# An LSTM's input operands on GpSimd beside first steps, weight sums queued in program order, and an output one gate later

## The chip, the cores and the metric

The kernel runs on one core of one Trainium2 chip. The metric is the device time of one execution in microseconds (us). A core has a matrix engine (TensorE, PE in the profile; its weight loads are PEld), a vector engine (VectorE, DVE), a scalar engine (ScalarE, ACT), a third elementwise engine (GpSimd, POOL) and a queue engine (SyncE, SP) that only issues transfers here. Each engine works through its own instructions in order; an instruction that waits for another engine or a transfer holds up all that stand behind it on its engine.

## The reference

The input x has 128 x 64 nodes of 256 features, all in float32. Four layers follow each other, each in the form x = x + layer(relu(layernorm(x))). The change lies in the first. After two graph convolutions that layer runs four LSTMs in turn, with window lengths p = 1 to 4:

```
for p in range(1, MAX_SKIP + 1):
    nw = Tv // p
    wins = h[:, :nw * p, :].reshape(Bv * nw, p, Hd)
    last = _lstm_last(Wih[p - 1], Whh[p - 1], bih[p - 1], bhh[p - 1], wins)
    idx = jnp.arange(nw) * p + (p - 1)
    h = h.at[:, idx, :].set(last.reshape(Bv, nw, Hd))
```

One step of an LSTM computes g = x_t @ Wih.T + h @ Whh.T + bias, splits g into the gates i, f, g, o, and then c = sigmoid(f) * c + sigmoid(i) * tanh(g) and h = sigmoid(o) * tanh(c). The state is zero at the start, so the first step has no h product and needs no gate f. The second layer is an attention over 512 edges, the third a graph convolution with batch norms, the fourth a dense attention.

## The kernel before

The 8192 tokens are four groups (g) of 2048. The LSTMs run over two halves: groups 0 and 1 through all four window lengths, then groups 2 and 3. Within a half a window length w is a phase; there are eight phases, numbered 0 to 7. A phase is a list of steps (class `Step`, L595): a part of a group, and a time t below w. Two parts are interleaved, so that the steps go first part t=0, second part t=0, first part t=1, and so on. A step has N columns: 512 for w=1, 256 for w=2 and 4, 336 for w=3.

A gate is a 2x2 block product done with seven products instead of eight (`gate`, L686; `product`, L644). Operand x[1] to x[7] of the seven are column blocks and sums of them. A step at t=0 has 3 gates of 7 products, a later step 4 gates of 14, since the state's seven products with Whh come on top. The profile holds a product as two matmul records. A gate goes through PSUM tiles pa (3 buffers), pb (2, shared with the transposes' `bank`) and pc (3); ScalarE copies pa (L694, L699) and pc (L702, for t=0 on VectorE), VectorE adds (L695, L705, L710), ScalarE applies the functions (L679, L732). `gate_done` (L714) makes the cell c (L728, L729, L731) and h with its own sums (L750 to L754), or writes the last h back into the node array hT (L737, L745).

The operands of a step are made by `prepare` (L617). For w above 1 these are two copies on ScalarE (L632 of two blocks, L633 of one) and three subtractions on VectorE (L634 of two blocks, L640 and L641 of one) into a tile xop with two buffers. The node array is read with a stride of w elements.

The main loop (L820) runs over slots, one gate per slot. Three gates are in flight: in a slot the new gate issues its first two products, the gate of two slots ago its last two, the gate of one slot ago its fifth, and the new gate two more. The next step's `prepare` is called beside the last gate but one of a step; for a new half's first step it is beside the last gate.

The weights (class `Weights`, L424) are a transfer of 1 MB on SP (L429) and four subtractions or additions on GpSimd (L440), giving tiles wih, sih for the input and whh, shh for the state. When a phase is over, `phase_over` (L806) loads the state weights of the next phase at once, and enters the input weights of the phase after next into a list that is served eight slots later (L863). wih has two buffers, whh one.

When a group is through w=4, `group_out` (L779) writes it out in two chunks (c = 0, 1): 16 transposes on PE (L167), four additions to the residual tiles xres on VectorE (L172), a store to xa on GpSimd's queue (L786), and, for the first half's groups, the loads of the next half's nodes hmem into hT on SP (L789). The main loop calls it one slot and two slots after the group's last gate. The residual tiles (4 buffers) are fetched on SP (L772). Outputs that are left when the slots end go into `last_outs` (L883); the attention layer then fetches their residuals (L919) and writes one of them out in each call of `edges` (L290). After the second call the pools of the LSTM's arrays are closed (L321) and the third layer's weights are loaded.

The order of each engine's instructions is not the program's alone: a planner takes them as its own estimate of the times lets them become ready. `late(ins)` ties an instruction behind the one that stands before it on its engine in the program. The first matmul of each group of products is tied in this way, so PE keeps the program's order; `prepare`, `Weights` and most of `gate` are not tied.

Of the kernel before, what the change touches and what calls it, by code (L numbers as in the profile page):

```python
# [13 lines left out]
ALU = mybir.AluOpType  # L14
# [3 lines left out]
T = 64  # L18
# [12 lines left out]
def gnn_stack_kernel(ctx: ExitStack, tc: tile.TileContext, a: dict, out: bass.AP):  # L31
    nc = tc.nc
# [45 lines left out]
    class Norm:  # L78


        def __init__(self, xt, root_on_scalar=False, keep=late):
            self.xt, self.root_on_scalar, self.keep, self.h = xt, root_on_scalar, keep, None
            self.st = stat.tile([P, 4, 6], F32, tag="ln_st", name="ln_st")
            self.mv = stat.tile([P, 4, 2], F32, tag="ln_mv", name="ln_mv")
# [170 lines left out]
    keep = tabs.tile([P, E], F32, tag="keep", name="keep")  # L255
# [159 lines left out]
    with ExitStack() as l0:  # L415
# [6 lines left out]


        class Weights:  # L424
            def __init__(self, kind, w):
                bufs = 2 if kind == "ih" else 1
                t = wsp.tile([P, 2, 4, 2, P], F32, tag=f"w{kind}", name=f"w{kind}", bufs=bufs)
                s = wsp.tile([P, 3, 4, P], F32, tag=f"s{kind}", name=f"s{kind}", bufs=bufs)
                nc.sync.dma_start(  # L429
                    out=t.rearrange("p k q j m -> p k (q j m)"), in_=a[f"W{kind}T"][:, w - 1]  # L430
                )
                a11, a12, a21, a22 = t[:, 0, :, 0, :], t[:, 1, :, 0, :], t[:, 0, :, 1, :], t[:, 1, :, 1, :]
                s1, s2, s4 = s[:, 0], s[:, 1], s[:, 2]
                for o, x, y, op in (
                    (s1, a21, a22, ALU.add),
                    (s2, s1, a11, ALU.subtract),
                    (s4, a12, s2, ALU.subtract),
                    (a21, a11, a21, ALU.subtract),
                ):
                    nc.gpsimd.tensor_tensor(o, x, y, op)  # L440
                self.of = {1: a11, 2: a12, 3: s4, 4: a22, 5: s1, 6: s2, 7: a21}

            def __call__(self, k, q):
# [6 lines left out]
        weights = {}  # L450


        with ExitStack() as conv:
# [43 lines left out]
            p = bank()  # L497
# [97 lines left out]
        class Step:  # L595
# [18 lines left out]
            def as_nodes(self, ap):  # L614
                return ap.rearrange("p q (b n) -> p q b n", n=self.nw) if self.w == 3 else ap

            def prepare(self):  # L617

                N, t = self.N, self.t
                x = xop.tile([P, 7 * NMAX], F32, tag="x", name="xop")  # L620
                if self.w == 1:
                    v = x[:, : 4 * N].rearrange("p (q n) -> p q n", n=N)
                    nc.vector.tensor_tensor(
                        v[:, 0:2], self.nodes(slice(2, 4), 0), self.nodes(slice(0, 3, 2), 0), ALU.subtract
                    )
                    b11, b21, b22 = (self.nodes(slice(k, k + 1), 0)[:, 0] for k in (0, 1, 3))
                    nc.vector.tensor_tensor(v[:, 2], b22, v[:, 0], ALU.subtract)
                    nc.vector.tensor_tensor(v[:, 3], b21, v[:, 2], ALU.subtract)
                    self.x = {1: b11, 2: b21, 3: b22, 4: v[:, 3], 5: v[:, 0], 6: v[:, 2], 7: v[:, 1]}
                    return  # L630
                v = x[:, : 7 * N].rearrange("p (q n) -> p q n", n=N)
                nc.scalar.copy(self.as_nodes(v[:, 0:2]), self.nodes(slice(0, 2), t))  # L632
                nc.scalar.copy(self.as_nodes(v[:, 2:3]), self.nodes(slice(3, 4), t))  # L633
                nc.vector.tensor_tensor(  # L634
                    self.as_nodes(v[:, 3:5]),
                    self.nodes(slice(2, 4), t),
                    self.nodes(slice(0, 3, 2), t),
                    ALU.subtract,
                )
                nc.vector.tensor_tensor(v[:, 5], v[:, 2], v[:, 3], ALU.subtract)  # L640
                nc.vector.tensor_tensor(v[:, 6], v[:, 1], v[:, 5], ALU.subtract)  # L641
                self.x = {1: v[:, 0], 2: v[:, 1], 3: v[:, 2], 4: v[:, 6], 5: v[:, 3], 6: v[:, 5], 7: v[:, 4]}

            def product(self, q, targets):  # L644
# [112 lines left out]
        steps, phases = [], []  # L757
        for half in range(2):
            ga, gb = 2 * half, 2 * half + 1
            for w in range(1, MAX_SKIP + 1):  # L760
                ph = len(phases)
# [54 lines left out]
        flight = []  # L816
        later, outs = [], []
        norm_steps = iter(())
        steps[0].prepare()
        for slot in range(len(tasks) + 2):  # L820
            new = tasks[slot] if slot < len(tasks) else None
            if slot == len(tasks):

                for _ in norm_steps:
                    pass
                first_hT = gp.tile([P, 4 * NMAX], F32, tag="gate", name="hT1_first")
                first_hT = first_hT[:, : 2 * CHUNK].rearrange("p (c t) -> p c t", c=2)
                for ip in range(2):
                    transpose_features(norms1[0].h, first_hT, ip, late)
            if new:  # L830
                step = steps[new[0]]
                one = step.gate(new[1])
                next(one)
            if len(flight) > 1:
                old = flight.pop(0)
                next(old[1], None)
                next(flight[-1][1])
            elif flight and not new:
                old = flight.pop(0)
                next(old[1], None)  # L840
            else:
                old = None
                if flight:
                    next(flight[-1][1])
            if new:
                next(one)
                flight.append((new, one))
                at, k = new[0], new[2]
                while outs and outs[0][0] <= slot:
                    group_out(*outs.pop(0)[1:])  # L850

                new_half = at + 1 < len(steps) and at and steps[at + 1].w == 1 < step.w
                if k == len(step.gates) - (1 if new_half else 2) and at + 1 < len(steps):
                    steps[at + 1].prepare()
                if step.w == MAX_SKIP and step.t == 2 and k < 2 and step.g < NGR - 1:
                    for u in range(2):
                        n = 4 * step.g + 2 * u + k
                        later.append((slot, "x", n))
            while later and later[0][0] <= slot:
                _, kind, n = later.pop(0)  # L860
                residual[n] = fetch_x(n)
            next(norm_steps, None)
            while later_weights and later_weights[0][0] <= slot:  # L863
                _, ph = later_weights.pop(0)
                weights["ih", ph] = Weights("ih", phases[ph])
            if old:
                (at, q, k), step = old[0], steps[old[0][0]]
                if k == len(step.gates) - 1:
                    if at + 1 == len(steps) or steps[at + 1].phase != step.phase:
                        phase_over(step.phase)  # L870
                    if step.phase == len(phases) - 1 and step.t == 1 and step.g == NGR - 1:

                        t_ = wsp.tile([P, 2, 4, 2, P], F32, tag="wih", name="x_first", bufs=2)
                        flat = t_.rearrange("p k q j m -> p k (q j m)")
                        norms1 = {}
                        for n in range(2):
                            xt = flat[:, n, :].rearrange("p (i d) -> p i d", i=4)
                            nc.sync.dma_start(out=xt, in_=xa[n])
                            norms1[n] = Norm(xt)
                        norm_steps = first_norms1(norms1)  # L880
                    if step.w == MAX_SKIP and step.t == MAX_SKIP - 1:
                        outs += [(slot + 1, step.g, 0), (slot + 2, step.g, 1)]
        last_outs = [(g, c) for _, g, c in outs]  # L883
    psums["banks"] = None

# [2 lines left out]
    with ExitStack() as l1:  # L888
# [306 lines left out]
        def sums(n, xt, keep=False):  # L1195

            st = stat.tile([P, 4, 6], F32, tag="ln_st", name="ln_st")
            mv = stat.tile([P, 4, 2], F32, tag="ln_mv", name="ln_mv")
            for i in range(4):
                ins = nc.vector.bn_stats(st[:, i, :], xt[:, i, :])  # L1200
                if keep and i == 0:
                    late(ins)
                nc.vector.bn_aggr(mv[:, i, :], st[:, i, :])
            rs, nm = w12t["x_rs"][:, n, :], w12t["x_nm"][:, n, :]
            ins = nc.gpsimd.tensor_scalar(rs, mv[:, :, 1], 1e-5, None, ALU.add)
            if keep:
                late(ins)
            nc.gpsimd.tensor_tensor(rs, rs, half_power, ALU.pow)
            nc.gpsimd.tensor_tensor(nm, mv[:, :, 0], rs, ALU.mult)
            nc.gpsimd.tensor_scalar(nm, nm, -1.0, None, ALU.mult)  # L1210
# [782 lines left out]
```

## Time and profile before

| what | value |
|---|---|
| median of 3 runs | 2067.21 us (2066.95 to 2071.63) |
| the profiled execution's own time | 2061.03 us |
| span of that execution | 2059.3 us |
| mean granted TensorE clock | 0.996 |
| first to last matmul of the LSTMs (L651) | 192.8 to 1273.5 us |
| PE busy in the span | 2006.1 us (97%) |
| POOL busy in the span | 308.2 us (15%) |

The span runs from the first to the last instruction; 1.7 us of the execution lie around it. A row such as `418.83 0.49 DVE L705 ...` is an instruction's start, its duration, its engine, its line in the kernel, what it writes and reads, and how many follow one another; in brackets stand the engine's idle time before it and what ended it. A wait such as `PE pa L651 <- DVE gate L705: 8.2, 11, 1.6` says that matmuls into pa waited for the instruction of L705, 8.2 us in all, 11 times, at most 1.6 us. The table by stages gives for each window the busy time and count for every engine, the clock and the share of the transfers' engines.

### The profile page before, as it was taken

How to read it: one execution, taken by the hardware profiler on the slowest of the kernel's cores; microseconds unless marked ns; L12 is line 12 of the kernel's file. 1: busy time of each engine (PE TensorE's matmuls, PEld its weight loads, DVE VectorE, ACT ScalarE, POOL GpSimd, SP SyncE). 2: the span in 40 equal slices, each digit the busy share in tenths (PEclk: the TensorE clock that was granted, in tenths of full speed). 3: DMA queues.
4: the chain of work that ended last, by engine and by line, in shares of the span. 5: the costliest groups of instructions: out<-in, count | busy, mean ns of one | idle time of the engine just before them, and what ended most of it. 6: DMA issues, size and time to landing. Idle time of an engine off the chain costs nothing. (4 is left out here: it accounts for less than half of the span.)

```text
span 2059.3 us, 25491 instructions
## 1 busy us (share of the span) xinstructions
PE 2006.1 (97%) x9444; PEld 1346.1 (65%) x9444; DVE 1359.5 (66%) x2507; ACT 1184.4 (58%) x2230; POOL 308.2 (15%) x416
## 2 busy tenths in 40 slices
PE   8999999999999999999999999999999999999998
PEld 6777478866688845887667887333334775444786
DVE  8755666564565477566556555677777877886776
ACT  4344766555565457566446564666675556591544
POOL 3000010020110020002001000323223420000563
PEclk9999999999999999999999999999999999999999
DMA  9331000100100170001001003412223841022012
GB/s 316 98 98 51 0 21 1 42 0 1 41 1 1 40 246 21 1 0 42 0 1 41 1 16 120 138 61 97 72 98 122 298 154 52 0 82 82 32 62 72
DMA packets 63196, 135.06 MB, mean 66 GB/s; under 512 B 6240, under 2 KB 40928, under 8 KB 60768
## 3 DMA queue, kind: packets, MB, share of 16 engines
q1 hardware_dynamic: 56832, 109.11, 15.6%
q0 software_dynamic: 5632, 24.12, 3.1%
q8 instruction: 74, 1.21, 0.2%
q14 instruction: 50, 0.41, 0.1%
q10 hardware_dynamic: 608, 0.20, 0.0%
HBM read 87.28 MB, written 46.14 MB: 65 GB/s over the span
## 5 line engine op out<-in xcount | busy, mean ns | idle before, releaser
L651 PE MATMUL pa<-xop,sih 128*128 128x256 f32 (+2 forms) x1056 | 344.4, 418 | 11.7 <-DVE gate L705 8.2
L679 ACT ACTIVATE gate<-gate,bias 128x256 f32<-128x256 f32 (+2 forms) x368 | 247.4, 679 | 173.6 <-DVE gate L695 91.0
L651 PEld LDWEIGHTS pa<-xop,sih 128*128 128x128 f32 x1056 | 198.4, 190 | 87.9 <-issue 22.8
L651 PE MATMUL pc<-xop,wih 128*128 128x256 f32 (+2 forms) x736 | 251.2, 423 | 0.0
L695 DVE TENSOR_TENSOR gate<-pb,gate 128x256 f32<-128x256 f32 (+2 forms) x184 | 87.5, 475 | 225.7 <-PE pb L651 154.1
L651 PE MATMUL pa<-lstm_h,shh 128*128 128x256 f32 (+1 forms) x672 | 212.7, 398 | 0.0
L993 DVE SCALAR_TENSOR_TENSOR lr<-lr 128x1024 f32<-128x1024 f32 x128 | 151.1, 1222 | 55.3 <-ACT lr L992 55.3
L651 PEld LDWEIGHTS pc<-xop,wih 128*128 128x128 f32 x736 | 139.8, 190 | 51.2 <-issue 23.0
L710 DVE TENSOR_TENSOR gate<-pc,gate 128x256 f32<-128x256 f32 (+2 forms) x184 | 87.6, 476 | 121.2 <-PE pc L651 120.9
L992 ACT COPY lr<-pair 128x1024 f32<-128x1024 f32 x128 | 123.1, 1014 | 47.6 <-PE pair L986 47.6
L651 PEld LDWEIGHTS pa<-lstm_h,shh 128*128 128x128 f32 x672 | 127.7, 190 | 30.2
L651 PE MATMUL pc<-lstm_h,whh 128*128 128x256 f32 (+1 forms) x448 | 141.8, 398 | 0.0
L694 ACT COPY gate<-pa 128x256 f32<-128x256 f32 (+2 forms) x184 | 76.1, 413 | 96.7 <-PE pa L651 96.1
L986 PE MATMUL pair<-sd_hot,xq 64*128 64x512 f32 x512 | 127.5, 616 | 0.3 <-ACT lr L992 0.3
L705 DVE TENSOR_TENSOR gate<-pa,gate 128x256 f32<-128x256 f32 (+2 forms) x184 | 87.5, 475 | 44.0 <-PE pa L651 43.4
L970 PE MATMUL bank<-wlv,hT 128*128 128x512 f32 x240 | 110.7, 604 | 0.0
L699 ACT COPY gate<-pa 128x256 f32<-128x256 f32 (+2 forms) x184 | 75.4, 410 | 59.1 <-PE pa L651 57.9
L679 ACT ACTIVATE gate<-pa,bias 128x256 f32<-128x256 f32 (+2 forms) x184 | 94.0, 511 | 23.6 <-PE pa L651 22.0
L440 POOL TENSOR_TENSOR sih<-wih 128x512 f32<-128x512 f32 x8 | 10.7, 1335 | 630.6 <-DMA wih<-in_WihT 484.4
L651 PE MATMUL pa<-xop,wih 128*128 128x256 f32 (+1 forms) x320 | 101.4, 398 | 2.7 <-ACT xop L632 2.7
L651 PE MATMUL pb<-xop,wih 128*128 128x256 f32 (+1 forms) x320 | 100.3, 398 | 0.4 <-DVE gate L695 0.4
L651 PEld LDWEIGHTS pc<-lstm_h,whh 128*128 128x128 f32 x448 | 85.1, 190 | 20.1
(346 smaller groups left out, 3809.2 us busy)
## 6 DMA issues: line engine op xcount, KB each, us to landing
field<-sd_hot SPq DMA_DIRECT2D x4, 2304.0 KB, 17.2
wih<-in_WihT SPq DMA_DIRECT2D x8, 1024.0 KB, 5.1
xres<-in_x SPq DMA_DIRECT2D x16, 512.0 KB, 4.6
xa<-xres POOLq DMA_DIRECT2D x16, 512.0 KB, 5.2
dense<-field POOLq DMA_DIRECT2D x4, 2048.0 KB, 8.5
xin<-xb SPq DMA_DIRECT2D x16, 512.0 KB, 3.4
h<-xb SPq DMA_DIRECT2D x16, 512.0 KB, 3.2
xin<-in_x SPq DMA_DIRECT2D x15, 512.0 KB, 3.9
```

The costliest lines, as they stand in the source:

```text
L440: nc.gpsimd.tensor_tensor(o, x, y, op)
L651: ins = nc.tensor.matmul(p[:, : self.N], weights[kind, self.phase](k, q), x[k], start=first_ and kind == "ih", stop=kind == "hh" or not se ...
L679: nc.scalar.activation(out, in_, AF.Tanh if q == 2 else AF.Sigmoid, bias=bias[:, self.w - 1, 2 * q + j : 2 * q + j + 1],)
L694: nc.scalar.copy(blk[0, 0], pa[:, :N])
L695: nc.vector.tensor_tensor(blk[0, 0], pb[:, :N], blk[0, 0], ALU.add)
L699: nc.scalar.copy(blk[1, 0], pa[:, :N])
L705: nc.vector.tensor_tensor(blk[1, 1], pa[:, :N], blk[1, 1], ALU.add)
L710: nc.vector.tensor_tensor(blk[1, 0], pc[:, :N], blk[1, 0], ALU.add)
L970: ins = nc.tensor.matmul(p, hTs[n][:, k, i * P : (i + 1) * P], wlv[:, k, :], start=k == 0, stop=k == 1)
L986: ins = nc.tensor.matmul(p[:, par, :], queries[it][r, c * P : (c + 1) * P], sd_hot[r, :], start=True, stop=True)
L992: nc.scalar.copy(lr, p)
L993: nc.vector.scalar_tensor_tensor(lr, lr, 0.2, lr, ALU.mult, ALU.max)
```

## The change

Three things change.

First, `prepare` is told the step beside which it runs. When that step has t=0 and w above 1, all five instructions are issued on GpSimd. The one exception is the second part's first step for w=3 and w=4 (its nodes come from the step just finished), which stays on ScalarE and VectorE. This moves the operands of 12 steps: for w=2 those of the second part's first step and of the first part's second step (four pairs of parts, 8 steps), for w=3 and w=4 those of the first part's second step (4 steps).

Second, the input weights that are served from the list are tied behind what precedes them on their engines: the load on SP and the four sums on GpSimd.

Third, a group's second chunk goes out three slots after its last gate, not two. For group 2 that slot is the first one past the last gate, where the loop writes nothing out; its second chunk is therefore left in `last_outs`, which holds three entries instead of two, and its two residual tiles are fetched again.

```
-                nc.sync.dma_start(
-                    out=t.rearrange("p k q j m -> p k (q j m)"), in_=a[f"W{kind}T"][:, w - 1]
+                keep(
+                    nc.sync.dma_start(
+                        out=t.rearrange("p k q j m -> p k (q j m)"), in_=a[f"W{kind}T"][:, w - 1]
+                    )
                 )
...
-                    nc.gpsimd.tensor_tensor(o, x, y, op)
+                    keep(nc.gpsimd.tensor_tensor(o, x, y, op))
...
-            def prepare(self):
+            def prepare(self, beside):
...
+                apart = beside is not None and beside.t == 0 and beside.w > 1
+                if apart and self.w > 2 and t == 0:
+                    apart = False
...
-                nc.scalar.copy(self.as_nodes(v[:, 0:2]), self.nodes(slice(0, 2), t))
-                nc.scalar.copy(self.as_nodes(v[:, 2:3]), self.nodes(slice(3, 4), t))
-                nc.vector.tensor_tensor(
+                copy = nc.gpsimd.tensor_copy if apart else nc.scalar.copy
+                sums = (nc.gpsimd if apart else nc.vector).tensor_tensor
+                copy(self.as_nodes(v[:, 0:2]), self.nodes(slice(0, 2), t))
+                copy(self.as_nodes(v[:, 2:3]), self.nodes(slice(3, 4), t))
+                sums(
                     self.as_nodes(v[:, 3:5]),
...
-                nc.vector.tensor_tensor(v[:, 5], v[:, 2], v[:, 3], ALU.subtract)
-                nc.vector.tensor_tensor(v[:, 6], v[:, 1], v[:, 5], ALU.subtract)
+                sums(v[:, 5], v[:, 2], v[:, 3], ALU.subtract)
+                sums(v[:, 6], v[:, 1], v[:, 5], ALU.subtract)
...
-                    steps[at + 1].prepare()
+                    steps[at + 1].prepare(step)
...
-                weights["ih", ph] = Weights("ih", phases[ph])
+                weights["ih", ph] = Weights("ih", phases[ph], late)
...
-                        outs += [(slot + 1, step.g, 0), (slot + 2, step.g, 1)]
+                        outs += [(slot + 1, step.g, 0), (slot + 3, step.g, 1)]
```

More of the change, by code (lines that the diff above doesn't have):

```diff
@@ L424, in gnn_stack_kernel, with __init__ @@
         class Weights:
-            def __init__(self, kind, w):
+            def __init__(self, kind, w, keep=lambda ins: None):
                 bufs = 2 if kind == "ih" else 1
@@ L818, in gnn_stack_kernel @@
         norm_steps = iter(())
-        steps[0].prepare()
+        steps[0].prepare(None)
         for slot in range(len(tasks) + 2):
```

## The prediction

> **What bounds the kernel now.** I read the page's first part, then the waits of PE over the LSTM stretch (192 to 1274 us), then a table by stages of the steps that the change touches, then the time line inside the worst.
>
> ```profile
> PE 2006.1 (97%) x9444; PEld 1346.1 (65%) x9444; DVE 1359.5 (66%) x2507; ACT 1184.4 (58%) x2230; POOL 308.2 (15%) x416
> ```
>
> PE is the bound of the whole, so an edit is worth what it takes from PE's idle time, at most 53 us everywhere. The waits of PE in the LSTMs:
>
> ```profile
> PE pa L651 <- DVE gate L705: 8.2, 11, 1.6
> PE bank L167 <- DVE xres L172: 5.3, 6, 3.1
> PE pa L651 <- ACT gate L694: 3.1, 4, 1.2
> PE pa L651 <- ACT xop L632: 2.7, 2, 1.3
> ```
>
> Few and short; weight loads behind the same gates add to them. Where they fall, the table by stages shows (window, length, then busy time and count of PE, PEld, DVE, ACT, POOL, clock, transfers):
>
> ```profile
> 264.00:275.10 11.10, 10.70 (x44) 7.61 (x43) 10.06 (x19) 9.56 (x18) 1.62 (x2) 1.00 0.28 95
> 333.40:342.40 9.00, 9.00 (x43) 7.88 (x42) 7.99 (x16) 6.76 (x16) 0.00 (x0) 1.00 0.00 0
> 342.40:351.80 9.40, 9.34 (x43) 7.90 (x43) 8.83 (x21) 7.77 (x18) 0.00 (x0) 1.00 0.01 3
> 412.70:427.00 14.30, 12.52 (x44) 7.77 (x43) 13.52 (x19) 9.55 (x17) 9.82 (x6) 1.00 0.00 0
> 565.80:577.40 11.60, 10.00 (x43) 7.65 (x42) 11.07 (x20) 7.81 (x17) 7.91 (x5) 1.00 0.00 1
> 712.20:734.60 22.40, 18.95 (x84) 13.44 (x83) 13.12 (x20) 6.43 (x13) 2.38 (x4) 0.92 0.79 258
> ```
>
> Each of the first five is one step at t=0. A product of 256 columns starts every 0.43 us (0.565 at 336), so 21 products want 9.03 us (11.86). What a window is longer than that is PE lost. DVE is busy 13.52 of 14.30 us and 11.07 of 11.60: in these steps VectorE sets the pace. Steps at t>0 run at pace (24.17 against 24.04).
>
> ```profile
> 416.73 2.17 DVE L634 TENSOR_TENSOR xop<-hT 128x672 f32<-128x672 f32 x1
> 417.90 2.15 POOL L440 TENSOR_TENSOR whh<-whh 128x512 f32<-128x512 f32 x1
> ...
> 421.40 1.57 DVE L640 TENSOR_TENSOR xop<-xop 128x336 f32<-128x336 f32 x1
> ...
> 426.29 0.83 PE L651 MATMUL pa<-xop,sih 128*128 128x336 f32 x2 [1.56 <-DVE gate L705]
> ```
>
> The operands stand in VectorE's queue ahead of the gate's additions, and each takes longer than alone (1.10 and 0.49 us) because GpSimd's weight sums run beside it.
>
> ```profile
> 720.61 1.23 DVE L623 TENSOR_TENSOR xop<-hT 128x1024 f32<-128x1024 f32 x1 [3.48 <-DMA hT<-hm]
> 724.89 1.25 PE L167 MATMUL bank<-ident,hT 128*128 128x128 f32 x8 [3.10 <-DVE xres L172]
> 725.98 1.64 PE L651 MATMUL pa<-hT,wih 128*128 128x512 f32 x2
> ```
>
> At the half's end VectorE waits for a load of new nodes, the output's additions stand behind, the output's second eight transposes find no bank, and after that idle time the clock is at half for 3.4 us (0.92 over the window).
>
> **Part one, the operands.** Excess over pace, first and second half: w=2, first pair of steps 2.1 and 2.9 (after 0.86 that the preceding step ends early); second pair 0.4 and 0.4; w=3, second first step, 2.4 and 2.4; w=4 likewise 2.6 and 1.9. Sum 15.1 us, the ceiling.
>
> Removed in a step at 256 columns: 1.1 us of ScalarE (0.66 and 0.43) and 1.5 of VectorE (0.68, 0.42, 0.41); at 336 columns 1.84 and, as the trace has them, 4.23 (2.17, 1.57, 0.49); at w=4 1.80 and 2.92 (2.10 and two of 0.41).
>
> Added on GpSimd: a 128x512 sum is 1.27 us (weights), a 128x256 one 0.72 (L136), a 128x512 one-input pass 0.77 (L1744), 128x256 0.56 (L1782): 0.77+0.56+1.27+0.72+0.72 = 4.0 us, 5.3 at 336 columns; with the longest rows (2.59 and 1.79 for sums, 1.08 and 0.84 for passes) 8.1. No row has GpSimd on strided nodes; these are the bounds, and I take 5 us, nearer the undisturbed rows. Is it in time? The buffer comes free when the last products of two steps ago are done, some 4.7 us into the step (338.1 in that of 333.4); the first two blocks are wanted 4.3 us later and the fifth product's block 6 us later. The copies are ready after 1.3 us, that block after 3.3 (six at the longest). So ScalarE's and VectorE's work gives way to work that is hidden; uncovered, 1 to 2 us a step.
>
> GpSimd also takes time from VectorE. Rows of before: of VectorE's two-SBUF-input work beside weight sums, L634 took 1.05 more, L640 up to 1.07, L731 0.11 to 0.65, L750 0.26 to 0.77; the additions that read PSUM (L695, L705, L710, L172) 0.00 to 0.03. What stays on VectorE and is exposed are L731 and the four of h, at 0.33 a time by the ten overlapped rows of L731 and L750; about half overlap, some 0.8 us a step against 1.5 to 4.2 removed. The Trainium skill, "GPSIMD Engine Reference", section Key points, says that GpSimd shares its SBUF interfaces with VectorE and contends with VectorE instructions that have two SBUF inputs. By that rule the trace agrees (2.17 against 1.10 us), and it speaks against the change; the first rival carries it.
>
> I take: w=2 first pairs 3.0 of 5.0 (thin margin on VectorE), second pairs nothing, w=3 4.0 of 4.8, w=4 3.4 of 4.5. Together 10.4; the ends are all of the 15.1, and the first rival's loss.
>
> **Part two, the weights.** At a phase's end the GpSimd queue now does the state's four sums first, then the operands, then the four input sums in a t=1 step, where VectorE has time. Before, eight sums run through both t=0 steps at the ends of phases 1, 2 and 5. At the end of phase 6 there are four alone, and that w=4 first step lost 2.8 instead of 3.8: 1.0 us gained once. The load of wih moves behind that of whh on SP; it is wanted a phase later (over 100 us; after phase 3 about 40, or 8 if the tie really holds it eight gates). The sums wait on GpSimd for that load with nothing urgent behind: the next operands come 30 us or more later. Cost 0; bounds 0 to 1 per phase end for VectorE held in the next step.
>
> **Part three, the second output.** Group 0: transposes at 720.75 to 725.98 move behind the next gate's products, whose nodes landed at 720.6. Kept are 2.5 us of transposes (as at 745.73); saved are 5.2-2.5 = 2.7 and 1.8 of clock (22.4 x 0.08), 4.5. Late next: the load into the second chunk, issued at 722 to 727, now at about 728 to 730, landing in 3.5 to 9.5; the next prepare read it at 736.9. VectorE may wait there up to 3.5, PE 0 to 2.5; I take 1.0, so 3.5 net. Group 1: nothing (its chunk is wanted 30 us later). Group 2: 2.83 us of transposes (1264.21 to 1267.04) move into the attention, where 16 take 1.8 to 2.3; gain 0.7. There VectorE is busy 7.7 of 10.2 us in the third round, and four more additions (2.5 us) fit. The two residuals fetched again (512 KB each, 4.7 us) run beside gates; the last pair of residuals must wait for the output in round one (about 1285) and lands by 1292, wanted at 1303. The third layer's weights come some 10 us later; the x load behind them has 20 us in hand.
>
> Sum: 10.4 + 1.0 + 3.5 + 0.7 = 15.6 us off 2061.0, that is 2045.4 in a run like the profiled one. The median shown stands 6.2 above that execution, so 2067.2 - 15.6 = 2051.6; I say 2052.
>
> **Rivals.** *Contention decides (slower).* Every one of VectorE's five two-input instructions in the 12 steps overlaps GpSimd and is held h. For w=2, 1.5 us are removed and about 0.8 spare (9.0 - 8.0 and 9.4 - 8.8 in the table): 8 x (5h - 2.3) is lost, the w=3 and 4 steps just keep their stalls, parts two and three give 5.2. At h = 0.85, between L731's 0.65 and L634's 1.05, that is 15.6 - 5.2 = +10: 2078. It is slower by 6 from h = 0.75. Against it: 0.33 was the mean.
>
> *Only the output pays.* The stalls are backlog of ScalarE and VectorE from the step before (the first pairs follow w=1) and the operands' places are taken by waits of L695 or L705 all the same: 5.2 plus 1, 2061. For it: DVE stays near 85% busy.
>
> *The attention's first loads stand behind the residuals.* If the planner leaves the x loads (1273.06) behind residuals that wait until 1285, chunk 2's statistics (1281.4) come at about 1292, and VectorE holds PE some 10 us: 2062. For it: the residual fetches are tied; against: the x loads are not, and are ready first.
>
> **How the numbers follow.** Forecast 0.64 (2045 to 2060); contention 0.13; only the output 0.14; loads 0.09. No change that can be told is within 0.3%, 6.2 us, 2061 to 2073. The two middle rivals fall about its edge, four parts in five inside. Faster 0.68, same 0.19, slower 0.13. Range: down to 2045 (15.1 + 1 + 4.5 + 1.1 = 21.7), up to 2068, past both middle rivals.
>
> **What would show it.** Right: no L634, L640, L641 on DVE in the 12 steps; the windows at 9.0 to 9.6 us (w=2, w=4 second) and under 12.4 (w=3), the waits on L705 and L694 mostly gone; no half clock at the half's end; three outputs in the attention. Wrong: waits of PE on xop from POOL; L731, L750 over 1.6 us in most steps; VectorE waiting for hT near 732, or for xin near 1281.

## The result, and the profile after

The changed kernel takes 2064.72 us (median of 9 runs, 2061.56 to 2066.38) against 2070.45 us for the kernel before on the same chip (9 runs, 2066.95 to 2072.51). The ratio is 0.9972 with a 95% interval of 0.9964 to 0.998: by the medians 5.7 us faster, where 15.6 were forecast. The time lies in the range given and at the faster edge of what was called no difference. On two other occasions the ratio was 0.9974 (0.9962 to 0.9985) and 0.9974 (0.9964 to 0.9984).

The experiments ran on three chips, called one, two and three below, and a kernel's own time differs between them by up to 9 us (before: 2062.2, 2070.4 and 2061.7 us). So ratios are taken on one chip only. The profiled execution of the change took 2064.72 us. That of before, shown above, took 2061.03 us, less than any of the nine timed executions of before, so it probably comes from another chip, and the two can't be subtracted. Stages inside them can.

In the changed kernel the lines from L429 on stand lower by 1 to 9: the products of L651 are at L660, L705 is L714, L731 is L740, L750 is L759, L632 to L641 are L641 to L650. The first part of the page:

```profile
PE 2013.3 (98%) x9444; PEld 1351.3 (66%) x9444; DVE 1354.5 (66%) x2471; ACT 1168.6 (57%) x2206; POOL 377.6 (18%) x476
```

GpSimd has 60 instructions and 69 us more, VectorE 36 fewer but only 5 us less: removing the rows of the 36 (0.4 to 2.2 us) had let more be expected. The waits of PE in the LSTMs, now 194 to 1265 us:

```profile
PE pa L660 <- DVE gate L714: 5.6, 9, 1.2
PE bank L167 <- DVE xres L172: 5.2, 5, 2.3
PE pa L660 <- ACT xop L641: 2.7, 2, 1.3
PE pa L660 <- DVE lstm_h L759: 1.2, 1, 1.2
```

The wait for ScalarE's gates (3.1 us) is gone, that for VectorE's additions fell only from 8.2 to 5.6, the output's did not move, and one is new: PE waits for h's product. The table by stages follows, in the order of the table of before (without its half's end). A last row is added for the second part's first step of w=4 in the second half:

```profile
265.20:275.70 10.50, 10.42 (x43) 7.73 (x42) 9.42 (x16) 8.67 (x16) 5.85 (x5) 1.00 0.29 101
333.45:342.50 9.05, 9.05 (x43) 7.98 (x42) 7.50 (x14) 6.35 (x15) 4.83 (x5) 1.00 0.00 0
342.50:351.90 9.40, 9.34 (x43) 7.82 (x42) 8.39 (x16) 6.89 (x15) 5.15 (x5) 1.00 0.01 3
412.80:425.65 12.85, 12.17 (x43) 7.82 (x42) 11.73 (x15) 7.94 (x15) 10.33 (x8) 1.00 0.00 0
563.50:574.70 11.20, 9.98 (x43) 7.63 (x42) 10.20 (x18) 7.03 (x16) 10.59 (x8) 1.00 0.00 0
1102.35:1115.10 12.75, 10.15 (x43) 7.57 (x42) 11.74 (x19) 7.00 (x16) 11.33 (x9) 1.00 0.00 0
```

Windows one and four are shorter (11.10 to 10.50, 14.30 to 12.85), two and three as they were, five hardly (11.60 to 11.20). The last is longer: the step took 10.9 us before and takes 12.75 now. In before, its window and its product of h (L750) read:

```profile
1110.10:1121.00 10.90, 9.74 (x44) 7.74 (x43) 10.25 (x23) 8.43 (x18) 2.42 (x2) 1.00 0.00 1
1116.20 1.25 DVE L750 TENSOR_TENSOR lstm_h<-gate 128x1024 f32<-128x1024 f32 x1
```

What happens there now, from the time line:

```profile
1107.26 1.19 POOL L641 COPY xop<-hT 128x512 f32<-128x512 f32 x1
1108.31 3.88 DVE L759 TENSOR_TENSOR lstm_h<-gate 128x1024 f32<-128x1024 f32 x1 [0.48 <-ACT gate L688]
1108.35 0.69 POOL L642 COPY xop<-hT 128x256 f32<-128x256 f32 x1
1108.96 2.15 POOL L643 TENSOR_TENSOR xop<-hT 128x512 f32<-128x512 f32 x1
1111.19 1.59 POOL L649 TENSOR_TENSOR xop<-xop 128x256 f32<-128x256 f32 x1
1112.25 0.70 PE L660 MATMUL pa<-lstm_h,whh 128*128 128x256 f32 x2 [1.23 <-DVE lstm_h L759]
1112.45 0.88 DVE L761 TENSOR_TENSOR lstm_h<-lstm_h 128x512 f32<-128x512 f32 x1
1114.58 0.70 PE L660 MATMUL pa<-xop,sih 128*128 128x256 f32 x2 [1.21 <-DVE gate L714]
```

The product of h takes 1.22 us where nothing runs beside it. Here it starts at 1108.31 and ends at 1112.19, that is 1.08 us after GpSimd's two-block subtraction ended (1111.11). So it did not run slowly all along: it waited for two GpSimd instructions in a row and then ran at full speed. In turn GpSimd's L649, 0.79 us alone, takes 1.59 as it starts while VectorE has its turn. PE waits for the product, and then for the gate's addition that stood behind it.

The half's end, where an idle PE and 3.4 us of half clock were to go:

```profile
724.52 1.23 DVE L737 TENSOR_TENSOR gate<-gate,lstm_c 128x1024 f32<-128x1024 f32 x1 [1.10 <-ACT gate L688]
725.78 1.22 DVE L738 TENSOR_TENSOR lstm_c<-gate 128x1024 f32<-128x1024 f32 x1
726.92 1.28 DVE L172 TENSOR_TENSOR xres<-bank,xres 128x512 f32<-128x512 f32 x2
727.66 1.25 PE L167 MATMUL bank<-ident,hT 128*128 128x128 f32 x8 [2.34 <-DVE xres L172]
733.78 1.23 DVE L630 TENSOR_TENSOR xop<-hT 128x1024 f32<-128x1024 f32 x1 [2.35 <-DMA hT<-hm]
758.11 1.25 PE L167 MATMUL bank<-ident,hT 128*128 128x128 f32 x8 [1.80 <-DVE xres L172]
```

The transposes moved behind the next gate's products as intended, but there they meet the last cell's two sums (L737, L738), which stand ahead of the output's additions on VectorE. The wait is 2.34 us instead of 3.10. Group 1's second output, 30 us later (758.11), was not expected to lose anything. There the additions stand behind two other instructions of VectorE (L630, operands, and L746, an h), and PE waits 1.80 us, 0.80 before.

### The profile page after: what moved, and what is told of

Its sections match the earlier page's. It is cut to its first block, busy times and chain, and to the rows that moved or that the text cites. A ratio compares the mean times of both kernels' runs of the same rounds, so it can differ in the third digit from the quotient of the medians.

```text
span 2062.9 us, 25539 instructions
## 1 busy us (share of the span) xinstructions
PE 2013.3 (98%) x9444; PEld 1351.3 (66%) x9444; DVE 1354.5 (66%) x2471; ACT 1168.6 (57%) x2206; POOL 377.6 (18%) x476
## 3 DMA queue, kind: packets, MB, share of 16 engines
q8 instruction: 74, 1.21, 0.2%
## 5 line engine op out<-in xcount | busy, mean ns | idle before, releaser
L660 PE MATMUL pa<-xop,sih 128*128 128x256 f32 (+2 forms) x1056 | 342.6, 417 | 5.9 <-DVE gate L714 5.6
L660 PE MATMUL pc<-xop,wih 128*128 128x256 f32 (+2 forms) x736 | 251.1, 423 | 0.0
L660 PEld LDWEIGHTS pa<-xop,sih 128*128 128x128 f32 x1056 | 198.6, 190 | 79.6 <-issue 19.9
L660 PE MATMUL pa<-lstm_h,shh 128*128 128x256 f32 (+1 forms) x672 | 212.7, 398 | 0.0
L660 PEld LDWEIGHTS pc<-xop,wih 128*128 128x128 f32 x736 | 139.8, 190 | 51.2 <-issue 23.0
L1001 ACT COPY lr<-pair 128x1024 f32<-128x1024 f32 x128 | 123.1, 1013 | 44.4 <-PE pair L995 43.6
L660 PEld LDWEIGHTS pa<-lstm_h,shh 128*128 128x128 f32 x672 | 127.7, 190 | 30.2
L660 PE MATMUL pc<-lstm_h,whh 128*128 128x256 f32 (+1 forms) x448 | 141.8, 398 | 0.0
L714 DVE TENSOR_TENSOR gate<-pa,gate 128x256 f32<-128x256 f32 (+2 forms) x184 | 87.3, 475 | 43.3 <-PE pa L660 42.7
L660 PE MATMUL pa<-xop,wih 128*128 128x256 f32 (+1 forms) x320 | 101.6, 399 | 2.8 <-ACT xop L641 2.7
L660 PE MATMUL pb<-xop,wih 128*128 128x256 f32 (+1 forms) x320 | 100.4, 398 | 0.0
L660 PEld LDWEIGHTS pc<-lstm_h,whh 128*128 128x128 f32 x448 | 85.1, 190 | 20.1
L995 PEld LDWEIGHTS pair<-sd_hot,xq 64*128 64x128 f32 x512 | 43.6, 185 | 72.7 <-issue 35.4
```

The source lines that it names most:

```text
L660: ins = nc.tensor.matmul(p[:, : self.N], weights[kind, self.phase](k, q), x[k], start=first_ and kind == "ih", stop=kind == "hh" or not se ...
L714: nc.vector.tensor_tensor(blk[1, 1], pa[:, :N], blk[1, 1], ALU.add)
L995: ins = nc.tensor.matmul(p[:, par, :], queries[it][r, c * P : (c + 1) * P], sd_hot[r, :], start=True, stop=True)
L1001: nc.scalar.copy(lr, p)
```

## Where the time went, term by term

For every step I took the time from its first product to the next step's first, less its number of products times the pace (0.43 us, 0.565 at 336 columns). The result is what the step is over pace. Neighbouring steps share a few products, so a row can hold a constant that no change gains (the first row's 6.7 is what the prediction counted as 5.0); only differences along a row count. Three profiles of before and three of the change (in order: the ones shown, and two from the experiments) give, in us:

| term | gain forecast | over pace, before | over pace, after | gain of the means |
|---|---|---|---|---|
| w=2, first pairs of steps | 3.0 | 6.7, 6.6, 6.5 | 3.7, 3.7, 5.2 | 2.4 |
| w=2, second pairs | 0 | 0.9 each | 0.9 each | 0 |
| w=3, first steps of both halves | 4.0 | 5.2, 5.0, 4.7 | 2.4, 2.7, 2.4 | 2.4 |
| w=4, second part's first step, and in half two the step behind it | 3.4 | 4.6, 4.6, 4.6 | 6.1, 4.3, 6.9 | -1.2 |
| w=4, first part's first step (weights) | 1.0 | 6.6, 6.7, 6.5 | 5.0, 5.0, 5.0 | 1.5 |
| half's end, with group 1's output | 3.5 | 15.0, 14.4, 14.6 | 13.8, 15.6, 13.9 | 0.2 |
| LSTMs' end | 2.8 | 7.6 each | 4.5 each | 3.0 |
| after the LSTMs | -2.1 | 785.8, 787.4, 787.0 in all | 789.6 in all (chip three alone) | -2.9 |

The gains add up to 5.4 us, the forecast to 15.6, and the timed differences are 5.7, 5.3 and 4.4. The LSTM stretch alone (first to last of its products) is 1080.7, 1079.9 and 1079.5 us before and 1070.6, 1070.9 and 1072.9 after, so single profiles of one kernel differ by 1 to 2 us. A part of that is the clock. In the third profile of the change the granted clock is at half from 1115.9 to 1119.3, after PE waited 1.97 us for VectorE, and about 1.1 us of the 6.9 in the fourth row comes from it. The half's end has such a stretch in the first two profiles of before and in the second of the change.

## The experiments

**The three parts one by one** (chip one, before 2062.19 us, 27 runs). The edits are the three parts of the change, each alone:

```
e1   -  weights["ih", ph] = Weights("ih", phases[ph], late)      (of the changed kernel)
     +  weights["ih", ph] = Weights("ih", phases[ph])
     -  outs += [(slot + 1, step.g, 0), (slot + 3, step.g, 1)]
     +  outs += [(slot + 1, step.g, 0), (slot + 2, step.g, 1)]
e2   -  apart = beside is not None and beside.t == 0 and beside.w > 1
     +  apart = False                            (and slot + 2 as in e1)
e3   apart = False, Weights without late, slot + 3 kept
```

> Part one alone: the operands of the 12 steps on GpSimd, weights and outputs as before. The LSTM stretch (first to last of its matmuls) was 1080.7 us before and 1070.6 us with the whole change. Theory, contention: the operands' gain at w=2 and w=3 is theirs, the loss at the second half's w=4 step too; the first pairs of w=2 gain about 3 us, w=3 about 2.8 us, w=4 loses 0 to 2 us, so the stretch is 1076 to 1078 us, and VectorE's h product (1.22 us alone) takes 1.6 us or more beside GpSimd at w=2 and 2.6 us or more at w=3 and 4. Rival, the sums: what was gained came from the weight sums' leaving the t=0 steps; then this kernel, where they stay and the operands queue behind them, gains nothing: 1080 to 1083 us.

> Part two alone: the input weights tied, operands on ScalarE and VectorE and outputs as before. Contention theory: 1 us at the first half's w=4 first step, up to 1.5 us at the two first pairs of w=2, where the sums ran beside VectorE's operands, and little at w=3, so the stretch is 1077.5 to 1079.5 us, time about 0.1% less. Rival, the sums: 4 us or more, 1074 to 1077 us.

> Part three alone: the second output a gate later. From the trace of the whole change: 2.1 us gained at the half's end (no half clock, but 2.3 us of waiting for a PSUM bank is left), 1.0 us lost at group 1's output, 3.0 us gained at the LSTM's end, so the stretch is 1076.6 us; 2.1 us of that come back as transposes in the attention and 1.3 us more where the norm's roots stand behind the third layer's weight sums on GpSimd, so the time is 0 to 1 us less than before. Rival, as forecast: 4 us less in time.

> The kernel before, unchanged, for a second profile. Its first profiled execution took 2061.03 us, below all nine timed runs (2066.95 to 2072.51). If the stretch of the LSTM is the same from run to run (1080.7 us within 0.5 us) and the difference lies in the attention's products with the edge field and in a halved clock, as in the profile of the changed kernel at 1576 to 1584 us, then the stretches, not the whole times of two profiles, are what is to be compared. If the LSTM stretch itself moves by some us, single profiles of it say little.

| kernel | median us | ratio to before | LSTM stretch | after it |
|---|---|---|---|---|
| before, again (profile alone) | 2062.28 | | 1079.9 | 787.4 |
| operands alone | 2062.67 | 1.0001 (0.9992 to 1.001) | 1083.6 | 786.3 |
| weights alone | 2063.19 | 1.0001 (0.9992 to 1.001) | 1080.3 | 785.9 |
| second output alone | 2065.29 | 1.0014 (1.0004 to 1.0023) | 1076.0 | 790.1 |

No part gains anything by itself. The operands alone were expected to gain most of what they gain in the whole; their stretch is 3.7 us longer instead, nearer to the rival's 1080 to 1083. Two lines of the waits of PE over its LSTM stretch say why:

```profile
PE pa L660 <- DVE gate L714: 6.7, 8, 2.0
PE pa L660 <- POOL xop L641: 5.1, 3, 2.2
```

The second is new: PE waits for GpSimd's copies. Without the ties all eight weight sums stand ahead of the operands in GpSimd's queue (at 575.28 PE waits 2.16 us for a copy that starts at 573.66, when the eighth sum is done). The granted clock is then at half from 576.2 to 579.6, and again from 1122.4 to 1125.8, which is a part of the 3.7. With the ties four sums do, and in the first trace of the changed kernel that wait does not occur. The weights alone gain 1.0 us in the first half's w=4 step, as forecast, and lose it in the step behind, where the four input sums now run beside VectorE's operands (the second part's step goes from 2.6 over pace to 3.8, and the w=3 pair of steps from 2.4 to 2.9). So the first two parts pay only together. This is read from the stretches: the parts alone change it by +3.7, +0.4 and -3.9 us, the whole by -6.7 (chip three) to -10.1 (the first profiles). No run has the first two parts without the third, and the whole did not run on chip one. The second output alone shortens the stretch by 3.9 us, as expected, and the attention gives back 2.7. Yet its timed runs lose 0.14% where up to 1 us of gain was expected. The profile doesn't show why, as the profiled execution (2060.99 us) is one of the two shortest of eleven.

**The whole, and group 0's output alone** (chip two, before 2070.41 us, 11 runs).

```
e7, e14   -  outs += [(slot + 1, step.g, 0), (slot + 3, step.g, 1)]
          +  outs += [(slot + 1, step.g, 0), (slot + (3 if step.g == 0 else 2), step.g, 1)]
```

> The changed kernel again, nothing edited, on the chip that ran the three parts one by one. The parts alone gave 1.0001, 1.0001 and 1.0014. If the parts were independent (rival), the whole would be no faster here: 1.001 to 1.002. My theory is that they are not: the operands fill GpSimd until the tied sums leave it, so the LSTM stretch should be 1070 to 1071.5 us as in the first trace of it, against 1083.6, 1080.3 and 1076.0 of the parts alone and 1079.9 of the kernel before, and the rest some 4 us longer for the second output that lies in the attention: 0.996 to 0.998 of before.

> The changed kernel, but only group 0's second output goes a gate later; groups 1 and 2 keep their places. My theory: the gain of part three lies at group 0 alone (the half's end, 2 us), and groups 1 and 2 pay. So group 1's output goes back to an excess of 2.9 (from 3.9), the LSTM's end to 7.6 (from 4.5): stretch about 1072.6, some 2 longer than with the change; the rest falls by some 4, to about 786, since no third output delays the norms' roots on GpSimd. Net 2 us faster than the change, 0.995 to 0.996 of before. Rival (the late output is worth its place everywhere and the loss in the attention is another's): the stretch grows by 2 and the rest stays where it is, 2 us slower than the change.

The change repeats: 2065.07 us, 0.9974 (0.9962 to 0.9985), stretch 1070.9. With only group 0's second output a gate later it is 2062.57 us, 0.9964 (0.9951 to 0.9978): stretch 1072.0, and after it 793.6 against 797.0. Group 1's output goes back from 3.9 to 2.9 over pace, the LSTMs' end from 4.5 to 7.6, as expected, and the attention gains more than that. The rival, by which the attention would stay as it is, falls. Against the whole change the median is 2.5 us lower, but the ranges of the two ratios overlap.

In the repeat of the change, the step that lost most in the first trace looks otherwise:

```profile
1107.47 1.28 POOL L442 TENSOR_TENSOR shh<-whh,shh 128x512 f32<-128x512 f32 x1
1108.50 1.32 DVE L759 TENSOR_TENSOR lstm_h<-gate 128x1024 f32<-128x1024 f32 x1 [0.48 <-ACT gate L688]
1108.69 2.10 POOL L641 COPY xop<-hT 128x512 f32<-128x512 f32 x1
1110.84 0.70 PE L660 MATMUL pa<-xop,wih 128*128 128x256 f32 x2 [0.43 <-POOL xop L641]
1111.82 2.30 POOL L643 TENSOR_TENSOR xop<-hT 128x512 f32<-128x512 f32 x1
1112.39 2.01 DVE L763 TENSOR_TENSOR lstm_h<-lstm_h 128x256 f32<-128x256 f32 x1
1115.04 0.70 PE L660 MATMUL pa<-xop,sih 128*128 128x256 f32 x2 [0.91 <-POOL xop L649]
```

Measured from the step's first product (1102.36 in the first trace, 1103.34 in this one) GpSimd's first copy starts 0.4 us later and h's product 0.8 earlier, so that the product is now ahead of the copy. It takes 1.32 us, and the copy is held (2.10 for 1.19); now the operands are late and PE waits 0.43 and 0.91 us for them. This step and the next are 2.1 us over pace, where before had 2.0 and the first trace of the change 3.9. Whichever engine comes first, the other pays, and either way the step gains nothing.

**The subtractions back on VectorE, and the loads' order** (chip two).

```
e6   -  sums = (nc.gpsimd if apart else nc.vector).tensor_tensor
     +  sums = (nc.gpsimd if apart and self.w == 2 else nc.vector).tensor_tensor
e9   -  nc.sync.dma_start(out=xt, in_=xa[n])              (first x loads, beside the last step of w=4)
     +  late(nc.sync.dma_start(out=xt, in_=xa[n]))
```

> The changed kernel, but for w=3 and w=4 GpSimd makes only the copies; the three subtractions go back to VectorE. If contention is what ate the gain there: h's product L759, which took 3.35 at w=3 and 2.66 and 3.88 at w=4, falls to at most 1.7, the excess of the second half's last w=4 step falls from 3.7 to at most 2, that of the first half's from 2.2 to 2 or less. Rival (VectorE's own load in these steps, and not GpSimd beside it, is what counts): the excess is as with the sums' move alone or worse, 3.5 at w=3, 3.8 and 1.9 at w=4, and L759 beside nothing still over 2. The copies before, on ScalarE, are the other possible bound: with them gone and the subtractions where they were, a fall of w=3 to 2 or less would show that they counted.

> The changed kernel, but the two loads of the next half's first nodes are tied as the weights are, so that the load of whh at the second half's w=4 may go ahead of them. There whh was issued at 1094.5 and its sums began 6.7 us later at 1101.2, against 4.7 in the first half. If the lateness of these sums is what puts the operands onto h's product there (3.88 us, excess 3.7): the sums begin some 2 us earlier, L759 falls to about 2.7 and the excess to about 2.2, as in the first half. Rival (the lateness is not the loads' doing, or the operands meet h's product whenever the sums start): sums not earlier, or excess still above 3.2.

The first is a miss of mine: 2080.61 us (one execution), stretch 1085.2. The w=3 steps rise from 1.0 to 4.7 us over pace (in the first of them PE waits 4.0 us in one piece for a gate's addition, L714), the first half's w=4 one from 2.2 to 5.1; the second half's lies at 2.4, within what the change itself has there (0.75 to 3.7). But h's product was not left alone as I had assumed: with the subtractions off GpSimd, the four input sums move up into the gap, and L759 takes 2.62 us at w=3 beside them (2.02 at w=4). So the run does not separate contention from load: h's product is still held, and VectorE has no room for its subtractions in these steps.

In the second the load of whh still stands between the two x loads on SP (1093.75, 1094.32, 1094.70), so the edit didn't do what it was for: the sums start 9.5 us after the first part's step began, 10.1 in the first trace of the change and 10.6 and 9.9 in two kernels that don't touch the loads. L759 takes 2.61 us for 3.88 and the excess is 2.15, but the first part's step ahead rises from 2.2 to 3.4, and the stretch is 1070.9: nothing won, and whether an earlier load would help stays open.

**GpSimd's subtraction twice, and all three beside one another** (chip three, before 2061.66 us, 14 runs).

```
e13  +  if apart:
     +      sums(self.as_nodes(v[:, 3:5]), self.nodes(slice(2, 4), t),
     +           self.nodes(slice(0, 3, 2), t), ALU.subtract)
```

> The changed kernel, but GpSimd makes its first subtraction L643 twice over (the same result written again): 1.5 us more of GpSimd in each of eight steps at w=2, 2.3 at w=3 and 2.1 at w=4, twice each. If GpSimd's time beside VectorE's two-input work is what costs: h's product and its three followers are held longer by about what is added there, so the excess of w=3 (1.0) rises to 2.5 or more, the first w=4 one (2.2) to 3.5 or more, the w=2 first pairs (1.5 and 0.4) to 2 and 1; stretch 4 to 10 us longer, and PE waits named after gate and lstm_h, none after xop. Rival one (GpSimd's work lies hidden): stretch within 1 us of the change. Rival two (it is late by its own slowness): PE waits for xop from GpSimd.

> The kernel before, nothing edited, in the same call as the changed one. Its timed runs had a median of 2062.2 on one chip and of 2070.4 on the other, the changed kernel 2065 on the latter; every profile of the whole change (chip two) shows PE short of instructions at about 1576 us (the products of L1167 in bursts, then 3.4 us of half clock), no profile of the parts alone or of before (chip one, and the first of all) shows it. If that stall is the chip's (theory), before shows it too on chip two, at L1158, with a rest after the LSTMs of about 795 us and a time near 2070, and does not on chip one. If it is the change's doing (rival), before has none on either chip, and its 8 us between chips lie elsewhere.

> The changed kernel again, beside before on one chip. If the stall is the chip's: 0.997 to 0.998 of before on either chip, stretch 1070 to 1071.5, and a rest some 4 us longer than before's in the same call; on chip one no bursts at 1576 and a time of about 2057. If it is the change's: bursts on either chip, and on chip one 1.001 to 1.002 of before, that is no gain at all.

> The changed kernel with only group 0's second output a gate later, again, beside the other two. If its gain over the change (2.5 us, 0.9964 of before on chip two) is the attention's and the second group's, as its trace there has it (group 1's output at an excess of 2.93 for 3.93, no wait for the roots), it repeats on any chip: 2 to 3 us under the change, 0.995 to 0.9965 of before.

The doubled subtraction is the experiment that shows the contention: 2065.30 us (one execution), stretch 1081.3 against 1072.9. The steps at w=3 rise from 1.0 to 2.6 and 2.4, the first w=4 one from 2.2 to 3.5, the w=2 ones behind L759 from 0.37 to 1.12. The time line of the first w=3 step (lines stand 7 further down here: L766 is L759, L768 is L761, L650 is the second subtraction):

```profile
418.56 2.31 POOL L643 TENSOR_TENSOR xop<-hT 128x672 f32<-128x672 f32 x1
418.95 3.33 DVE L766 TENSOR_TENSOR lstm_h<-gate 128x1344 f32<-128x1344 f32 x1
420.94 3.51 POOL L650 TENSOR_TENSOR xop<-hT 128x672 f32<-128x672 f32 x1
422.62 2.55 DVE L768 TENSOR_TENSOR lstm_h<-lstm_h 128x672 f32<-128x672 f32 x1
426.78 1.03 PE L667 MATMUL pa<-xop,sih 128*128 128x336 f32 x2 [2.07 <-DVE gate L721]
```

The four take turns: h's product (1.55 alone) waits for the first subtraction, the second waits for the product, h's next sum (1.15 in the changed kernel) waits for the second, and PE at the end waits for the gate's addition. No wait for xop from GpSimd appears in this kernel, so it isn't lateness. Summed over the LSTMs, VectorE's instructions beside GpSimd's take 35.5 us longer than the shortest of the same line and shape, against 27.3 in the changed kernel on this chip and 17.3 in before: 8.2 us more held time, and 8.4 us more stretch. That the two are so near is in part luck. Two waits in this kernel end in 3.4 us of half clock (427.3 and 1123.6), one in the change, so up to 1.7 us of the 8.4 is clock, and not all of the held time reaches PE.

The rest: before 2061.39 us in this profile, stretch 1079.5 and 787.0 after it; the change 2057.28 us, 0.9974 (0.9964 to 0.9984), 1072.9 and 789.6; with group 0's output alone 2054.11 us, 0.9968 (0.9956 to 0.998), 1072.0 and 787.6. The last has the lowest median again, as on chip two, 3.2 us under the change; its ratio had been expected at 0.995 to 0.9965. The ratios, 0.9968 and 0.9974, lie nearer to each other than the medians and their intervals overlap, so the gain over the change is likely but not shown clear of noise. Laid product by product upon before of the same chip, the change is 5.6 us ahead at the LSTMs' end, 3.4 after the transposes at 1304, and 2.2 after 1318. The second loss is seen on GpSimd, in the change:

```profile
1307.18 0.23 POOL L99 TENSOR_SCALAR ln_rs<-ln_mv 128x4 f32<-128x4 f32 x1
1307.38 0.72 POOL L136 TENSOR_TENSOR w1S<-w1S,w1T 128x256 f32<-128x256 f32 x1
1308.07 1.70 POOL L136 TENSOR_TENSOR w1T<-w1T 128x256 f32<-128x256 f32 x1
1309.73 1.70 POOL L136 TENSOR_TENSOR w1S<-w1T,w1S 128x256 f32<-128x256 f32 x1
1311.40 1.04 POOL L100 TENSOR_TENSOR ln_rs<-ln_rs,half_power 128x4 f32<-128x4 f32 x1
```

and with group 0's output alone:

```profile
1298.45 0.22 POOL L99 TENSOR_SCALAR ln_rs<-ln_mv 128x4 f32<-128x4 f32 x1 [0.32 <-DVE ln_mv L88]
1298.75 1.04 POOL L100 TENSOR_TENSOR ln_rs<-ln_rs,half_power 128x4 f32<-128x4 f32 x1
```

The third output holds the LSTM's arrays for a call longer; the third layer's weights, which take their place, come late (their first sum starts at 1305.91, at 1299.59 in before and 1291.66 with group 0's output alone), and their sums (L136) fall between two instructions of a norm's root: 4.2 us from L99 to L100 instead of 0.3. PE then waits 1.0 us for ScalarE (L1001).

## Why the prediction was wrong

**Right.** The operands at w=2: 3.0 us forecast, 2.9 in the first two traces of the change, 1.4 in the third; the second pairs gain nothing. GpSimd's time a step, taken as 5, is 4.9 to 6.1 at w=2, and the work lies hidden there in the first two traces. That is not safe: in the third a last h of w=1 (L746, 1.21 us alone) meets GpSimd's operands (809.17 to 811.15), and PE waits for the gate's addition behind it:

```profile
809.44 2.79 DVE L746 TENSOR_TENSOR hT<-gate 128x1024 f32<-128x1024 f32 x1
812.62 0.70 PE L660 MATMUL pa<-xop,sih 128*128 128x256 f32 x2 [1.59 <-DVE gate L714]
```

The weights' 1.0 us appears to the tenth in the first half's w=4 step (3.8 to 2.8), and 0.5 more in the second half's. VectorE waits 2.35 us for the second chunk's nodes (up to 3.5 had been said) at no cost to PE. The attention's x loads were not held back; that rival did not happen. The LSTMs' end gains 3.0 and the 16 transposes come back at 2.1, as worked out.

**Step one that failed: "w=4 3.4 of 4.5".** It came to -1.2. The term in it that was mis-sized is "at 0.33 a time [...] about half overlap, some 0.8 us a step". What is held is not each instruction by a third of a microsecond but h's product by whole GpSimd instructions: in the first trace 0.42 and 0.52 us at w=2, 1.8 at w=3, 1.44 and 2.66 at w=4, and its three followers another 0.4 to 1.2 us together. VectorE is held 2.6 to 3.0 us in a step at w=3 or 4, not 0.8. Where the hold falls differs from one trace to the next: the first half's w=4 step gains 0.4 in all three, the second half's, with the step behind it, loses 1.9, nothing and 2.7 (1.1 of it half clock). The mean came from weight sums beside L731, which pays little; the operands land on L759, the last link to the next step's state products. I also had GpSimd's operands at 5 us where w=3 takes 7.6 (1.13, 0.66, 2.35, 2.11, 1.39) and w=4 6.7 to 7.1. At w=2 the hold of L759 is smaller and fits into VectorE's slack. So the rival "Contention decides" had the mechanism. Its price of 0.85 us was too low for h's product at w=3 and 4, but it let five instructions in 12 steps pay it, and the product is held in eight; so its 2078 us didn't come either.

**Step two: "w=3 4.0 of 4.8".** It came to 2.4, by the same hold: 3.35 us for 1.55, then the gate's addition late by 0.7 us to PE.

**Step three: "saved are 5.2-2.5 = 2.7 and 1.8 of clock (22.4 x 0.08), 4.5. [...] so 3.5 net" at the half's end.** It came to 0.2. I named the load that might be late next, which cost nothing, and not the two cell sums of 2.45 us on VectorE into which the moved output runs; and I gave group 1 nothing, which loses 1.0 against two of the three profiles of before (the third has a wait of 1.93 us there too). The 1.8 of clock was no fixed cost either: of three profiles of before one has no half clock at the half's end, and of three of the change one has it (727.8 us, 3.4 us long).

**Step four: "the third layer's weights come some 10 us later"**, costed at nothing. They come 6.3 us later than in before (1305.91 for 1299.59) into a GpSimd queue that a norm's root shares: 1.3 us on the same chip, the second loss above.

By the table's means these steps miss 4.6, 1.6, 3.3 and 0.6 us (the last with the LSTMs' end, 0.7 forecast and 0.1 found), 10.1 together; with 0.6 missing at w=2 and 0.5 more than forecast from the weights it is the 10.2 between 15.6 and 5.4. The signs named beforehand said so: L750's successor is over 1.6 us in all eight steps of the first trace, the windows of w=3 and w=4 stay above what was asked (12.85 for 12.4, 11.20 for 9.6).

The Trainium skill, "Trainium Architecture — The Big Picture", section What this means for kernel authors, says that the port pair that VectorE and GpSimd share is an exclusive lock and not a split of bandwidth. The trace agrees: L759 ends 1.08 us after the GpSimd instruction that it waited for, whole and at full speed. Priced by that rule, with one subtraction of two blocks (2.1 to 2.4 us in these rows) waited for in each of the four steps, 8.4 to 9.6 us would have stood against the 7.4 that the forecast gave to them; they brought 1.2.

## What to carry to other kernels

Here, work that was moved to GpSimd stayed hidden from PE as long as VectorE had slack. Where it met, in time, a two-input VectorE instruction on the recurrence's path (the chain from one step's h to the next step's products) and no slack was left, the price was one or two whole GpSimd instructions. So look at what VectorE does in the stretch where the moved work will run, and not at the average hold. When a transfer or an output is moved in an order, list what already stands on every engine at the new place, GpSimd and the cell's sums too. And parts of a change can be worth nothing alone and something together, as one makes room in the queue that the other needs: a part's own run is not its share.

## What the runs showed that was not expected

A GpSimd copy with one input holds VectorE's two-input product as well: L759 waited through L642, and in the repeat the copy L641 was held in turn (2.10 us for 1.19). Additions that read PSUM are untouched: 0.00 to 0.03 us longer beside GpSimd in every trace. What is held in these traces are VectorE's instructions with two inputs from SBUF.

GpSimd's rows grow with the nodes' stride. The copy of 512 columns takes 0.66 us at w=2 (8 bytes from one element to the next) and 1.19 at w=4 (16 bytes), 1.8 times; 672 columns at w=3 (12 bytes) take 1.13, 1.3 times as long per element as at w=2. The subtraction of two blocks goes from 1.50 to 2.15 us, 1.4 times. The Trainium skill, "GPSIMD Engine Reference", section Performance pitfalls for Q7 kernels, gives about half more per element beyond 8 bytes; here it lies between 1.2 and 1.8 times.

On chip two, and in the first profile of the change, whose before had the same 2070.45 us, all five profiles (two of the change, three of kernels that differ from it by one line) have PE idle at one place of the attention without a wait that the profile names ("issue"); that PE is short of instructions there is a guess. Rows of the first profile of the change at the place, then the same line on chip three:

```profile
1576.74 0.34 PE L1167 MATMUL pair<-att,xv_in 64*64 64x64 f32 x5 [0.39 <-issue]
1577.49 0.35 PE L1167 MATMUL pair<-att,xv_in 64*64 64x64 f32 x5 [0.41 <-issue]
```

```profile
1577.38 1.16 PE L1167 MATMUL pair<-att,xv_in 64*64 64x64 f32 x64
```

The products come in bursts of about five every 0.73 us, and then the granted clock is at half for 3.4 us; the part after the LSTMs takes 797 and 798.4 us in the change there and 789.6 on chip three. That before pays the same on chip two is argued from its times (2070.4 there, 2061.7 and 2062.2 elsewhere) and the unchanged ratio; before was not profiled on that chip. Why the chip does it stays open, as does why the change's timed runs on chip three fall into two sets (2052.9 to 2055.7 and 2057.2 to 2058.7 us).
